# A tensor per strip, strips' rows and sums loaded once, in layer 1 of a two-layer graph network

## The chip, the cores and the metric

The kernel runs on one core of a Trainium2 chip. The metric is the time of one execution in microseconds on the device. Beside the time of a run stands the span of its profile, from the first to the last instruction; the profiled execution's time is a little longer than its span.

## The reference

Two layers over a graph of 3327 nodes with 128 features each, and a sparse 3327 x 3327 adjacency with weights. Layer 0 is a graph attention layer with four heads, layer 1 a graph convolution. Cut to what matters:

```
h = jnp.maximum(_layernorm(x, axis=-1), 0.0)
x = x + gatv2(h, adj, w1, w2, a, Wlin, w)        # per head: softmax-like weights over neighbours,
                                                 # then weights @ h @ Wlin.T, leaky relu, concat @ w
h = jnp.maximum(_layernorm(x, axis=-1), 0.0)
A_t = adj + jnp.eye(n)
D_inv = A_t.sum(axis=1) ** (-0.5)
HW = h @ W.T + b
x = x + jax.nn.relu((D_inv[:, None] * A_t * D_inv[None, :]) @ HW)
```

The change touches the last line alone: the product of the whole adjacency with HW, the scaling, the relu, and the sum with layer 0's output.

## The kernel before

**Tiles.** The nodes are padded to 3328 and cut into 26 blocks of 128 (NB = 26). Layer 0 runs block by block: for each block it gathers the neighbours' rows from a table in HBM (L595, on GpSimd), computes scores on TensorE and VectorE (L622 to L657), weighs the rows (L670, L690), and closes the block (`close`, L744 to L812). Closing block b makes its new rows xn = x + layer 0's output (L786), stores them to the HBM tensor `xn_d` (L788, from SP's queue), and puts D_inv * HW of the block into `x_sb[:, b]` (L811), from where layer 1 takes it.

**Layer 1 in strips.** Layer 1 works on strips of four blocks (512 nodes; NS = 7 strips, the last of two blocks). The sum for strip s over all columns j of the adjacency is a chain of matmuls that adds up in one PSUM bank, x_sb[:, j] times the 128 x 512 tile (s, j) of the transposed adjacency, which layer 0 left in the HBM tensor `AT_d`. A column of a strip can only be added when its block is closed. So the sum of a strip comes in three parts:

- `part1`: while block b of strip s was being prepared in layer 0, the columns that were closed by then (`finished(b)` of them: none for strip 0, 2 for strip 1, 6, 10, 14, 18, 22 for the others) were summed (`known_step`, L375) and stored to the HBM tensor `part1_d` (L387).
- `part2`: during the last two blocks of layer 0, `begin` (L920) adds twelve more columns for strips 1, 2 and 3 (L942), copies each sum out of PSUM (L947, ScalarE) into the tile `outT` and stores it to the HBM tensor `part2_d` (L948, SP).
- the rest: `layer1` (L995) goes through the list `work` of 74 pairs (s, j). The first 36 (`in_front`) are strip 0's columns 0 to 24 and strip 1's columns 14 to 24, which need no block 25; they run between the instructions that close block 25. Then come column 25 of strips 0 and 1, and strips 2 to 6. Each pair is one matmul of 128 x 512 (L1006; two records in the profile).

The 74 tiles are brought from `AT_d` in seven pieces of eleven (`strip`, L911), each into one of four buffers `g`; the DMAs of a piece alternate between SP's and GpSimd's queue (L916). A piece is fetched when the buffer's last reader is through: the fourth when the last gathered rows have been weighed (L670), the next when columns 0 to 10 are done, and so on (`allow("g")`).

**A strip's end.** `strip_in` (L955) is called some columns before a strip ends. It takes two buffers of layer 0's ring tiles, `r0` (three) and `r1` (two), and loads from SP's queue the strip's new rows (L961, from `xn_d`), its part1 (L963) and, for strips 1 to 3, its part2 (L965). `strip_out` (L968) then adds the parts to the PSUM sum (L973, L975; strip 0 has no part, there a copy on ScalarE, L977), turns the result with four transposes (L982), adds the block's own x_sb (L983), multiplies by D_inv (L984), takes the relu and adds the new rows (L985), and stores to the output from ScalarE's queue (L986). It is a generator: its first piece is emitted with the next pair of the list, its transposes two pairs later.

**What sets the order.** All of it is emitted inside `tc.manual_schedule()`: each engine executes its instructions, and each queue issues its DMAs, in the order in which the Python emits them; waits for other engines and for DMAs are put in as semaphore waits ahead of the instruction. `slot()` (L879) is called between the stages of layer 0 and moves every generator in flight by one step: closing and finishing blocks, preparation, fetching, `begin`. When the last block's groups are done, `slot()` and one pair of `layer1` alternate until all blocks are closed.

Of the kernel before, what the change touches and what calls it, by code (L numbers as in the profile page):

```python
# [231 lines left out]
def _sparse_layers(tc, nc, x, adj, w1, w2, a, wlin, w, gw, gb, gb_sb, gwT, x_sb, dinv, flag, ident, out):  # L232
# [24 lines left out]
    with ExitStack() as l0:  # L257
# [4 lines left out]
        xn_d = dram.tile([NP, D], F32, name="xn_d")  # L262
        part1_d = dram.tile([D, NP], F32, name="part1_d")
        part2_d = dram.tile([D, NP], F32, name="part2_d")
        NS = -(-NB // 4)
        TURN = NP * P + HALF
# [86 lines left out]
        def prep(b, k):  # L353
# [21 lines left out]
            def known_step(j0, js, at):  # L375
                assert all(blks[j0 + q].closed for q in js)
                pq = bank()
                for q in js:
                    nc.tensor.matmul(pq[:, :P], x_sb[:, j0 + q, :], at[:, q, :], start=(q == 0), stop=(q == js[-1]))  # L379
                yield  # L380
                if j0 == 0:
                    k.part1 = pb.tile([P, P], F32, name="part1", bufs=1)
                    nc.scalar.copy(k.part1, pq[:, :P])
                else:
                    nc.vector.tensor_add(k.part1, k.part1, pq[:, :P])
                if j0 + len(js) == finished(b):
                    nc.sync.dma_start(part1_d[:, b * P:(b + 1) * P], k.part1)  # L387
# [7 lines left out]
            SOME = 8 + 4 * 32  # L395
# [348 lines left out]
        def close(k, hb):  # L744
# [43 lines left out]
            nc.sync.dma_start(xn_d[b * P:(b + 1) * P, :], xn)  # L788
# [37 lines left out]
        NCODE = 20  # L826
        NLIST = 42
# [66 lines left out]
        strips = {}  # L894
        early = {s: range(finished(4 * s), finished(4 * s) + BEGUN) for s in (1, 2, 3) if finished(4 * s) + BEGUN < NB - 3}
# [24 lines left out]
        def begin():  # L920
# [5 lines left out]
            thirds = pa.tile([P, NP], F32, name="adjb")[:, :3 * PAIR * BANK].rearrange("p (k j i) -> p k j i", k=3, j=PAIR)  # L926

# [10 lines left out]
            for i, (s, j) in enumerate(work):  # L938
                assert blks[j].closed
                if j == early[s][0]:  # L940
                    po = bank()
                nc.tensor.matmul(po, x_sb[:, j, :], thirds[:, i // PAIR % 3, i % PAIR], start=(j == early[s][0]), stop=(j == early[s][-1]))  # L942
                if i % PAIR == PAIR - 1:
                    bring(i // PAIR + 3)
                if j == early[s][-1]:
                    part2 = pv.tile([P, H, P], F32, name="outT").rearrange("p h i -> p (h i)")
                    nc.scalar.copy(part2, po)  # L947
                    nc.sync.dma_start(part2_d[:, 4 * s * P:4 * s * P + BANK], part2)  # L948
                for _ in range(4):
                    yield  # L950
# [4 lines left out]
        def strip_in(s):  # L955

            n = min(4, NB - 4 * s)
            r0 = pr.tile([P, 2, BANK], F32, name="r0", bufs=3).rearrange("p k (b d) -> p k b d", b=4)[:, :, :n]
            r1 = pr.tile([P, 2, BANK], F32, name="r1").rearrange("p k (b d) -> p k b d", b=4)[:, :, :n]
            rows = slice(4 * s * P, (4 * s + n) * P)  # L960
            nc.sync.dma_start(r0[:, 0], xn_d[rows, :].rearrange("(b p) d -> p b d", p=P))  # L961
            if finished(4 * s):
                nc.sync.dma_start(r1[:, 0], part1_d[:, rows].rearrange("p (b i) -> p b i", b=n))  # L963
            if s in early:
                nc.sync.dma_start(r0[:, 1], part2_d[:, rows].rearrange("p (b i) -> p b i", b=n))  # L965
            return n, rows, r0, r1

        def strip_out(s, po, n, rows, r0, r1):  # L968

            ot, t, xo = r0[:, 1], r1[:, 1], r0[:, 0]  # L970
            po = po[:, :n * P].rearrange("p (b i) -> p b i", b=n)
            if s in early:
                nc.vector.tensor_add(ot, po, ot)  # L973
            if finished(4 * s):
                nc.vector.tensor_add(ot, ot if s in early else po, r1[:, 0])  # L975
            elif s not in early:
                nc.scalar.copy(ot, po)  # L977
# [5 lines left out]
            nc.vector.tensor_add(t, pt[:, :n, :], x_sb[:, 4 * s:4 * s + n, :])  # L983
            nc.vector.tensor_tensor(t, t, dinv[:, 4 * s:4 * s + n, None].to_broadcast([P, n, D]), OP.mult)  # L984
            nc.vector.scalar_tensor_tensor(xo, t, 0.0, xo, op0=OP.max, op1=OP.add)  # L985
            nc.scalar.dma_start(out[rows, :].rearrange("(b p) d -> p b d", p=P), xo)  # L986
# [8 lines left out]
        def layer1():  # L995
            ending, sums, ins = [], {}, {}
            for i, (s, j) in enumerate(work):
                if i == in_front:
                    yield "all"
                w = min(4, NB - 4 * s) * P  # L1000
                if s not in sums:
                    sums[s] = ps_z.tile([P, 2, BANK], F32, name="z")[:, 0]
                if j == min(NB - 1, first_column(s) + 4 * (s not in front)):
                    assert len(ending) < 2
                    ins[s] = strip_in(s)
                nc.tensor.matmul(sums[s][:, :w], x_sb[:, j, :], strips[s, j][:, :w], start=(j == first_column(s)), stop=(j == NB - 1))  # L1006
# [3 lines left out]
                if j == NB - 1:  # L1010
                    ending.append(strip_out(s, sums.pop(s), *ins.pop(s)))
# [370 lines left out]
```

## Time and profile before

| | us |
|---|---|
| three runs | 2480.82, 2483.68 (median), 2485.28 |
| the profiled execution's own time | 2484.15 |
| its span | 2482.0 |
| PE busy in the span | 2226.6 (90%) |
| DVE, POOL, ACT busy | 2053.7 (83%), 1769.7 (71%), 639.7 (26%) |
| layer 1's first matmul (L1006) starts at | 2388.8 |
| its last starts at | 2471.9 |
| last load of `AT_d` for layer 1 issued (SP) | 2436.01 to 2437.48 |
| last store of the output issued (ScalarE) | 2476.3 |

PE is TensorE, DVE VectorE, ACT ScalarE, POOL GpSimd and SP SyncE; PEld is the loading of weights. A name with q, as in SPq, is the engine's sequencer, which issues DMAs and waits. Rows of the timeline give the start, the length, engine, line, operation, output and inputs, how many, and in brackets the engine's idle time before it and who ended it. The mean granted clock of TensorE over the span is 0.981 of full speed. The page's row of DMA shares shows the 16 DMA engines at 90% or more in all but the last of 40 slices.

### The profile page before, as it was taken

Reading aid. Unit: us, or ns where it says so; the run is one execution under the profiler, and the core shown is the slowest. Engines: PE = TensorE matmul, PEld = TensorE weight load, DVE = VectorE, ACT = ScalarE, POOL = GpSimd, SP = SyncE. Lnnn points to the kernel's source line nnn. Section 1 sums busy time; section 2 is a strip of 40 time slices with the busy share of each in tenths; the row PEclk is TensorE's granted clock in tenths of the full one; section 3 lists DMA queues with packets and bytes.
Section 4 is the critical chain, followed back from the end, with each engine's and each line's share of the span. In section 5 each row is a group of like instructions: output and inputs, shape, how many; then the busy total and the mean of one; then the engine's idle time right before and its main releaser. Section 6 shows DMA issues by size and latency. Waiting matters only on the chain.

```text
span 2482.0 us, 51942 instructions
## 1 busy us (share of the span) xinstructions
PE 2226.6 (90%) x19254; PEld 1594.8 (64%) x19254; DVE 2053.7 (83%) x6426; ACT 639.7 (26%) x1547; POOL 1769.7 (71%) x1867
## 2 busy tenths in 40 slices
PE   6589889989988998998999999899999999999996
PEld 4466666666666766766666666666667667666653
DVE  7688988888898888889889888988988888896633
ACT  4122232223222222222222222232222222221110
POOL 3577777777777777777777777777777777777750
PEclk9799999999999999999999999999999999999998
DMA  9999999999999999999999999999999999999996
GB/s 302 381 342 332 350 333 323 352 344 316 334 368 325 323 352 334 323 345 358 324 327 360 336 323 348 353 322 338 358 329 316 354 336 319 340 334 329 367 304 174
DMA packets 401715, 826.93 MB, mean 333 GB/s; under 512 B 38435, under 2 KB 270383, under 8 KB 398127
## 3 DMA queue, kind: packets, MB, share of 16 engines
q0 software_dynamic: 144464, 628.85, 71.9%
q1 hardware_dynamic: 165343, 147.87, 18.9%
q10 hardware_dynamic: 91648, 46.80, 6.3%
q8 instruction: 155, 2.54, 0.4%
q14 instruction: 105, 0.86, 0.1%
HBM read 754.47 MB, written 113.22 MB: 350 GB/s over the span
## 4 chain that ended last, share of the span: by engine, by line
PE 41%; DVE 27%; DMA 16%; POOL 9%; issue 5%; SPq 1%; ACT 1%; DVEq 0%; POOLq 0%; ACTq 0%
DVE r L638 14%; PE z L622 14%; DMA g<-table,idx 11%; PE s L657 10%; POOL g L595 9%; DVE cand L422 3%; PE ag L670 2%; PE z L627 2%; PE tr L379 2%; DVE codes L410 1%; DVE cand L456 1%; DVE lists L453 1%; DMA g<-AT_d 1%; PE tr L942 1%; PE z L1124 1%
## 5 line engine op out<-in xcount | busy, mean ns | idle before, releaser
L595 POOL DMA_INDIRECT g<-table,idx x1664 | 1615.9, 971 | 575.1 <-issue 412.1
L638 DVE TENSOR_TENSOR r<-z,x1n 128x1024 f32<-128x1024 f32 x832 | 1010.7, 1215 | 136.5 <-PE z L622 134.4
L622 PE MATMUL z<-ident,g 128*128 128x128 f32 x6656 | 926.0, 279 | 106.9 <-DVE r L638 97.7
L622 PEld LDWEIGHTS z<-ident,g 128*128 128x128 f32 x6656 | 754.5, 143 | 244.2 <-DVE r L638 145.7
L657 PE MATMUL s<-r,sel 128*4 128x512 f32 (+1 forms) x3744 | 507.3, 582 | 9.9 <-DVE r L638 9.5
L657 PEld LDWEIGHTS s<-r,sel 128*4 128x4 f32 x3744 | 86.4, 86 | 256.2 <-issue 181.0
L698 ACT COPY ssb<-s 128x512 f32<-128x512 f32 x208 | 121.9, 586 | 497.0 <-PE s L657 496.5
L422 DVE MAX8 cand<-codes 128x8 f32<-128x52 uint16 x1664 | 217.5, 205 | 0.0
L670 PEld LDWEIGHTS ag<-g,wt 128*32 128x32 f32 x3328 | 116.7, 110 | 102.5 <-issue 95.7
L670 PE MATMUL ag<-g,wt 128*32 128x133 f32 x3328 | 158.4, 278 | 0.0
L730 ACT ACTIVATE sc<-sc 128x32 f32<-128x32 f32 x208 | 47.9, 230 | 413.3 <-DVE sc L725 252.8
L633 DVE TENSOR_TENSOR r<-z,x1n 128x128 f32<-128x128 f32 x104 | 30.1, 289 | 150.0 <-PE z L627 147.5
L367 ACT COPY at<-tr 128x512 f32<-128x512 f32 (+1 forms) x175 | 97.1, 555 | 218.0 <-PE tr L365 205.5
L453 DVE MAX8 lists<-cand 128x8 f32<-128x272 f32 (+1 forms) x338 | 133.3, 394 | 2.2
L365 PE MATMUL tr<-ident,adjb 128*128 128x128 f32 x676 | 108.4, 283 | 25.2 <-DMA adjb<-in_adj_dram 15.6
L635 ACT ACTIVATE r<-z 128x512 f32<-128x512 f32 x104 | 62.1, 597 | 256.4 <-DVE r L633 256.4
L709 PE MATMUL tr<-ident,ssb 128*128 128x128 f32 x832 | 124.9, 273 | 1.8 <-ACT ssb L698 1.8
L627 PE MATMUL z<-oi,x1b 128*128 128x256 f32 x416 | 124.3, 381 | 0.0
L595 POOL DMA_INDIRECT ge<-table,idxo x104 | 98.5, 947 | 32.9 <-issue 13.1
L456 DVE MATCH_REPLACE8 cand<-lists,cand 128x272 f32<-128x272 f32 (+1 forms) x312 | 118.0, 378 | 0.0
L410 DVE SCALAR_TENSOR_TENSOR codes<-adjb,code 128x832 uint16<-128x832 f32 x104 | 104.3, 1019 | 12.7 <-DMA adjb<-in_adj_dram 12.7
L379 PE MATMUL tr<-at,x_sb 128*128 128x128 f32 x488 | 72.2, 287 | 38.4 <-DVE sc L725 31.4
(200 smaller groups left out, 2451.8 us busy)
## 6 DMA issues: line engine op xcount, KB each, us to landing
adjb<-in_adj_dram SPq DMA_DIRECT2D x26, 1664.0 KB
table<-AT_d SPq DMA_DIRECT2D x26, 1664.0 KB
AT_d<-at ACTq DMA_DIRECT2D x150, 256.0 KB
g<-table,idx POOLq DMA_INDIRECT x1664
table<-img SPq DMA_DIRECT2D x12, 1296.0 KB
adjb<-AT_d SPq DMA_DIRECT2D x72, 128.0 KB
g<-AT_d SPq DMA_DIRECT2D x25, 256.0 KB
g<-AT_d POOLq DMA_DIRECT2D x25, 256.0 KB
```

Source lines behind the costliest of these rows:

```text
L410: nc.vector.scalar_tensor_tensor(codes[:, i], adjb[:, c0:c0 + part], 0.0, code[:, c0:c0 + part], op0=OP.not_equal, op1=OP.mult, accum_out= ...
L422: nc.vector.max(cand[:, c, 8:].rearrange("p (r s) -> p r s", s=32)[:, :, sgm % 32], codes.rearrange("p a b -> p (a b)")[:, sgm % 32 * SEG: ...
L453: nc.vector.max(top, of)
L456: nc.vector.match_replace(out=of, in_to_replace=top, in_values=of, imm_value=0.0)
L595: return nc.gpsimd.indirect_dma_start(out=g[:, t, lo:hi], out_offset=None, in_=tab, in_offset=bass.IndirectOffsetOnAxis(ap=at[:, t:t + 1], ...
L622: nc.tensor.matmul(z[:, i, q * P:(q + 1) * P], g[:, m % 2 * 4 + q, c0:c0 + D], ident, is_transpose=True, start=(q == 0 or m < 8), stop=(m ...
L627: nc.tensor.matmul(z[:, i, :n], k.x1b[:, h * D:(h + 1) * D], k.oi[:, hb * n:(hb + 1) * n], start=False, stop=True, skip_group_check=True)
L638: nc.vector.tensor_tensor(r.rearrange("p h (i s) -> p h i s", s=16), z.rearrange("p h (i s) -> p h i s", s=16), k.x1n[:, 2 * hp:2 * hp + 2 ...
L657: nc.tensor.matmul(k.s[32 * h:32 * h + 4, :n], sel[:, h, 31 - row:35 - row], r[h // 2][:, h % 2, :n], start=(row == 0), stop=(last and (m ...
L670: nc.tensor.matmul(k.ag[32 * cg:32 * cg + 32, u, :WORK], wt[:, t].rearrange("p h q -> p (h q)"), g[:, t, f0:f0 + WORK], start=(w == 0 and ...
L698: nc.scalar.copy(ssb, s)
L709: nc.tensor.transpose(pt[:, q, :], ssb[:, q * P:(q + 1) * P], ident)
```

## The change

- `xn_d` and `part1_d` become a list of HBM tensors each, one per strip, of 128 x 512, so that a strip's new rows or sums are one contiguous row per partition. The stores L387 and L788 write a 128-wide part of such a row; they stay on SP's queue.
- `part2_d` is gone. What `begin` has summed stays in SBUF, in three places that layer 0's preparation no longer uses (the tiles `codes`, `cand` and `lq`).
- `strip_in` is gone. When `layer1` starts, `places` takes four ring buffers at once (eight places of 128 x 512), one for each strip's new rows and one for strip 0's sum, and issues the loads of the new rows of strips 0 to 5 from ScalarE's queue. `parts` takes the tile `adjb`, once `begin` is through, and issues the loads of part1 of strips 1 to 6 from ScalarE's queue.
- The part2 of a strip is added to its loaded part1 in SBUF by VectorE: strip 1's four pairs before the end of the front, those of strips 2 and 3 two pairs after the strip's first column.
- The new rows of the last strip are loaded from ScalarE's queue at the first pair after the front, when block 25 is closed.
- `strip_out` has one add for a strip with a part, and works in place in the strip's two places.

The name `sums` in `layer1` becomes `acc`. The diff:

```diff
--- before.py
+++ after.py
@@ -259,10 +259,8 @@
         dram = l0.enter_context(tc.tile_pool(name="dram", bufs=1, space=bass.MemoryType.DRAM))
         tables = [dram.tile([(NP + 1) * ROW], F32, name=f"table{k}") for k in range(2)]
         hT_d = dram.tile([P, NP], F32, name="hT_d")
-        xn_d = dram.tile([NP, D], F32, name="xn_d")
-        part1_d = dram.tile([D, NP], F32, name="part1_d")
-        part2_d = dram.tile([D, NP], F32, name="part2_d")
         NS = -(-NB // 4)
+        xn_d, part1_d = ([dram.tile([P, 4 * P], F32, name=f"{name}{s}") for s in range(NS)] for name in ("xn_d", "part1_d"))
         TURN = NP * P + HALF
         AT_d = dram.tile([NB * TURN], F32, name="AT_d")
         w1_sb = res.tile([P, H, D], F32, name="w1_sb")
@@ -384,7 +382,7 @@
                 else:
                     nc.vector.tensor_add(k.part1, k.part1, pq[:, :P])
                 if j0 + len(js) == finished(b):
-                    nc.sync.dma_start(part1_d[:, b * P:(b + 1) * P], k.part1)
+                    nc.sync.dma_start(part1_d[b // 4][:, b % 4 * P:(b % 4 + 1) * P], k.part1)
 
             known = []
 
@@ -392,7 +390,6 @@
                 known[:] = [f for f in known if next(f, "end") != "end"]
 
 
-            SOME = 8 + 4 * 32
             cand = pb.tile([P, 2, SOME + 4 * 32], F32, name="cand", bufs=1)
             tab_at = 0
             while b == 0 and tab_at < NB:
@@ -785,7 +782,7 @@
             st = pb.tile([P, 1], F32, name="st")
             nc.vector.scalar_tensor_tensor(xn, x_sb[:, b, :], 1.0, py[:, 0, :], op0=OP.mult, op1=OP.add, accum_out=st)
             nc.vector.tensor_scalar(st, st, -1.0 / D, None, op0=OP.mult)
-            nc.sync.dma_start(xn_d[b * P:(b + 1) * P, :], xn)
+            nc.sync.dma_start(xn_d[b // 4][:, b % 4 * P:(b % 4 + 1) * P], xn)
             yield
 
             two = pv.tile([P, 2, D], F32, name="agn")
@@ -824,6 +821,7 @@
         ENDS = {1: (0,), 3: (1,), 5: (2,), 8: (3, 4)}
         ROWS = {1: (0, True), 3: (0, True), 5: (0, True), 7: (0, False), 8: (2, True)}
         NCODE = 20
+        SOME = 8 + 4 * 32
         NLIST = 42
         NPREP = 72
         SLOTP = 6 * 2 * NG
@@ -892,6 +890,7 @@
         PAIR = 2
         BEGUN = 12
         strips = {}
+        xs, sums, part2 = {}, {}, {}
         early = {s: range(finished(4 * s), finished(4 * s) + BEGUN) for s in (1, 2, 3) if finished(4 * s) + BEGUN < NB - 3}
 
         def columns(v, part):
@@ -924,6 +923,8 @@
             if not work:
                 return
             thirds = pa.tile([P, NP], F32, name="adjb")[:, :3 * PAIR * BANK].rearrange("p (k j i) -> p k j i", k=3, j=PAIR)
+            room = (pa.tile([P, NP // 4], F32, name="codes")[:, :BANK], pb.tile([P, 2 * (SOME + 4 * 32)], F32, name="cand", bufs=1)[:, :BANK],
+                    pb.tile([P, BANK], F32, name="lq", bufs=1))
 
             def bring(k):
                 if k < len(pairs):
@@ -943,47 +944,59 @@
                 if i % PAIR == PAIR - 1:
                     bring(i // PAIR + 3)
                 if j == early[s][-1]:
-                    part2 = pv.tile([P, H, P], F32, name="outT").rearrange("p h i -> p (h i)")
-                    nc.scalar.copy(part2, po)
-                    nc.sync.dma_start(part2_d[:, 4 * s * P:4 * s * P + BANK], part2)
+                    part2[s] = room[len(part2)].rearrange("p (b i) -> p b i", b=4)
+                    nc.scalar.copy(part2[s], po.rearrange("p (b i) -> p b i", b=4))
                 for _ in range(4):
                     yield
 
         def first_column(s):
             return early[s][-1] + 1 if s in early else finished(4 * s)
 
-        def strip_in(s):
-
-            n = min(4, NB - 4 * s)
-            r0 = pr.tile([P, 2, BANK], F32, name="r0", bufs=3).rearrange("p k (b d) -> p k b d", b=4)[:, :, :n]
-            r1 = pr.tile([P, 2, BANK], F32, name="r1").rearrange("p k (b d) -> p k b d", b=4)[:, :, :n]
-            rows = slice(4 * s * P, (4 * s + n) * P)
-            nc.sync.dma_start(r0[:, 0], xn_d[rows, :].rearrange("(b p) d -> p b d", p=P))
+        def blocks_of(s):
+            return min(4, NB - 4 * s)
+
+        def rows_of(s):
+
+            n = blocks_of(s)
+            nc.scalar.dma_start(xs[s], xn_d[s][:, :n * P].rearrange("p (b d) -> p b d", b=n))
+
+        def places():
+
+            held = [pr.tile([P, 2, BANK], F32, name=f"r{i // 3}", bufs=3 - i // 3) for i in range(4)]
+            slots = [t[:, i].rearrange("p (b d) -> p b d", b=4) for t in held for i in range(2)]
+            assert NS < len(slots)
+            xs.update((s, slots[s][:, :blocks_of(s)]) for s in range(NS))
+            if not finished(0):
+                sums[0] = slots[NS][:, :blocks_of(0)]
+            for s in range(NS - 1):
+                rows_of(s)
+
+        def parts():
+
+            of = [s for s in range(NS) if finished(4 * s)]
+            kept = pa.tile([P, NP], F32, name="adjb")[:, :len(of) * BANK].rearrange("p (s b d) -> p s b d", b=4, d=D)
+            for i, s in enumerate(of):
+                n = blocks_of(s)
+                sums[s] = kept[:, i, :n]
+                nc.scalar.dma_start(sums[s], part1_d[s][:, :n * P].rearrange("p (b i) -> p b i", b=n))
+
+        def strip_out(s, po):
+
+            n, ot, xo = blocks_of(s), sums[s], xs[s]
+            po = po[:, :n * P].rearrange("p (b i) -> p b i", b=n)
             if finished(4 * s):
-                nc.sync.dma_start(r1[:, 0], part1_d[:, rows].rearrange("p (b i) -> p b i", b=n))
-            if s in early:
-                nc.sync.dma_start(r0[:, 1], part2_d[:, rows].rearrange("p (b i) -> p b i", b=n))
-            return n, rows, r0, r1
-
-        def strip_out(s, po, n, rows, r0, r1):
-
-            ot, t, xo = r0[:, 1], r1[:, 1], r0[:, 0]
-            po = po[:, :n * P].rearrange("p (b i) -> p b i", b=n)
-            if s in early:
                 nc.vector.tensor_add(ot, po, ot)
-            if finished(4 * s):
-                nc.vector.tensor_add(ot, ot if s in early else po, r1[:, 0])
-            elif s not in early:
+            else:
                 nc.scalar.copy(ot, po)
             yield
             yield
             pt = ps_tr.tile([P, 4, P], F32, name="tr")
             for k in range(n):
                 nc.tensor.transpose(pt[:, k, :], ot[:, k, :], ident)
-            nc.vector.tensor_add(t, pt[:, :n, :], x_sb[:, 4 * s:4 * s + n, :])
-            nc.vector.tensor_tensor(t, t, dinv[:, 4 * s:4 * s + n, None].to_broadcast([P, n, D]), OP.mult)
-            nc.vector.scalar_tensor_tensor(xo, t, 0.0, xo, op0=OP.max, op1=OP.add)
-            nc.scalar.dma_start(out[rows, :].rearrange("(b p) d -> p b d", p=P), xo)
+            nc.vector.tensor_add(ot, pt[:, :n, :], x_sb[:, 4 * s:4 * s + n, :])
+            nc.vector.tensor_tensor(ot, ot, dinv[:, 4 * s:4 * s + n, None].to_broadcast([P, n, D]), OP.mult)
+            nc.vector.scalar_tensor_tensor(xo, ot, 0.0, xo, op0=OP.max, op1=OP.add)
+            nc.scalar.dma_start(out[4 * s * P:(4 * s + n) * P, :].rearrange("(b p) d -> p b d", p=P), xo)
 
 
         front = range(min(2, NS - 1))
@@ -993,22 +1006,28 @@
         pieces = [work[i:i + PIECE] for i in range(0, len(work), PIECE)]
 
         def layer1():
-            ending, sums, ins = [], {}, {}
+            ending, acc = [], {}
+            places()
             for i, (s, j) in enumerate(work):
                 if i == in_front:
                     yield "all"
-                w = min(4, NB - 4 * s) * P
-                if s not in sums:
-                    sums[s] = ps_z.tile([P, 2, BANK], F32, name="z")[:, 0]
-                if j == min(NB - 1, first_column(s) + 4 * (s not in front)):
-                    assert len(ending) < 2
-                    ins[s] = strip_in(s)
-                nc.tensor.matmul(sums[s][:, :w], x_sb[:, j, :], strips[s, j][:, :w], start=(j == first_column(s)), stop=(j == NB - 1))
+                if state["early"] is None and NS - 1 not in sums:
+                    parts()
+                for t in early:
+                    if i == work.index((t, first_column(t))) + 2 and t not in front or i == in_front - 4 and t in front:
+                        nc.vector.tensor_add(sums[t], sums[t], part2[t])
+                w = blocks_of(s) * P
+                if s not in acc:
+                    acc[s] = ps_z.tile([P, 2, BANK], F32, name="z")[:, 0]
+                if i == in_front:
+                    assert blks[NB - 1].closed
+                    rows_of(NS - 1)
+                nc.tensor.matmul(acc[s][:, :w], x_sb[:, j, :], strips[s, j][:, :w], start=(j == first_column(s)), stop=(j == NB - 1))
                 if i % PIECE == PIECE - 1 or i == len(work) - 1:
                     allow("g")
                 ending[:] = [f for f in ending if next(f, "end") != "end"]
                 if j == NB - 1:
-                    ending.append(strip_out(s, sums.pop(s), *ins.pop(s)))
+                    ending.append(strip_out(s, acc.pop(s)))
                 yield "one"
             for e in ending:
                 for _ in e:
```

## The prediction

> **What bounds the kernel now.** I read the page first, then the stretches of the span, the queue of SP in order of time, the chain of waits, and ACT and PE row by row near the end. The page gives averages over a kernel whose first 2389 us the change hardly enters; the stretches cut out the stage that it does enter.
>
> ```profile
> 2300.00:2340.00 40.00, 39.88 (x326) 26.41 (x325) 26.82 (x60) 7.59 (x23) 30.25 (x33) 1.00 1.06 364
> 2340.00:2360.00 20.00, 20.00 (x153) 13.51 (x143) 10.99 (x24) 3.71 (x10) 14.19 (x16) 1.00 1.05 368
> 2412.00:2424.00 12.00, 12.00 (x38) 5.98 (x37) 3.25 (x17) 1.31 (x5) 7.91 (x12) 1.00 1.09 291
> 2430.00:2441.00 11.00, 0.05 (x1) 0.00 (x0) 1.20 (x2) 0.00 (x0) 0.00 (x0) 0.70 1.09 298
> 2455.00:2472.00 17.00, 17.00 (x51) 8.53 (x50) 5.62 (x9) 0.00 (x0) 0.00 (x0) 1.00 0.34 105
> ```
>
> Columns: length, busy time of PE, PEld, DVE, ACT, POOL, granted clock, DMA share, GB/s. Until 2424 PE is always busy and the DMA engines are full. From 2430 to 2441 PE stands, at a clock of 0.70, while the DMA engines are still full. After 2455 PE is the bound and the DMA engines are two thirds idle. So layer 1 has one hole, of 11 us. SP's queue says why.
>
> ```profile
> 2397.15 2.69 SPq L961 DMA_DIRECT2D r<-xn_d  x1
> 2400.20 32.92 SPq L916 DMA_DIRECT2D g<-AT_d  x24
> 2433.17 0.82 SPq L961 DMA_DIRECT2D r<-xn_d  x1
> 2434.34 0.44 SPq L963 DMA_DIRECT2D r<-part_d  x1
> 2434.83 0.42 SPq L965 DMA_DIRECT2D r<-part_d  x1
> 2435.37 0.36 SPq L788 DMA_DIRECT2D xn_d<-xn  x1
> 2436.01 1.47 SPq L916 DMA_DIRECT2D g<-AT_d  x3
> ...
> 2441.24 1.11 PE L982 MATMUL tr<-ident,r 128*128 128x128 f32 x4 [11.20 <-DVE r L975]
> ```
>
> Strip 1's new rows and sums (L961, L963, L965) stand behind 24 loads of the adjacency, and PE's transposes of strip 1 wait for them. Right behind them stands the store of block 25's new rows, L788, whose data DVE had ready at 2416.3. What holds SP is in the chain of waits:
>
> ```profile
> 2402.08 7.15 DMA g<-AT_d
> 2409.24 0.02 issue
> 2409.25 0.50 SPq L916
> ...
> 2418.29 14.04 DMA g<-AT_d
> 2432.34 0.78 SPq L916
> ...
> 2434.83 4.85 DMA r<-part_d
> ```
>
> An issue at 2409.25 waited for the landing of the one at 2402.08, that at 2432.34 for the one at 2418.29: each time eight issues earlier. ACT's stores are in the same count: the first L986's semaphore wait ends at 2438.4, when the L961 of 2433.17 lands, eight DMAs before it in program order. So SP and ACT together have at most eight DMAs open.
>
> **The change, part by part.** Durations are of this execution, span 2482.0, whose time is 2484.15; the median of the runs shown is 2483.68, so I add the sum to the median.
>
> *Bytes moved ahead.* ACT issues six loads of new rows (6 x 0.262 MB) and six of sums (5 x 0.262 + 0.131 MB) when layer 1 begins, about 2389.5: 3.015 MB into full DMA engines. No row shows such loads there. Bounds: nothing, if they fill holes; 10.3 us at the 294 GB/s of 2412 to 2441. I take 8.2 us, from the 366 GB/s of 2300 to 2360, since these loads have 2 KB rows and the adjacency's have 512 B ones, nearer to the gathers of that stretch.
>
> *Bytes removed ahead of L788.* The third store of L948 at 2389.41, L961 at 2397.15, and the three of strip 1: 5 x 0.262 = 1.311 MB at 294 GB/s, 4.5 us. The other stores and loads that go lie under a full PE (2300 to 2360, 2442 to 2472) and cost nothing today.
>
> *ACT's queue.* The twelve issues come after L698 (ends 2389.5) and ahead of L730 and L732.
>
> ```profile
> 2388.91 0.58 ACT L698 COPY ssb<-s 128x512 f32<-128x512 f32 x1 [0.81 <-PE s L657]
> 2390.98 0.24 ACT L730 ACTIVATE sc<-sc 128x44 f32<-128x44 f32 x1 [1.49 <-DVE sc L727]
> ...
> 2398.87 0.66 PE L670 MATMUL ag<-g,wt 128*32 128x133 f32 x16
> ```
>
> An ACT issue takes 0.37 us (L370, 175 of them), so alone they cost 4.4 us, and L670 has that much room. But each waits for the landing eight DMAs before it. The seventh and eighth wait for the last two SP loads of the third piece, which land at 2402.5 and 2403.4 by the trace's semaphores. Then ACT is free at 2405.3 at the earliest; at 2410.3 if seven of the loads (1.84 MB, 5.0 us) push those landings back. I take 2407.5. From L730 to the end of L664 it takes 0.97 us, so L670 starts at 2408.5, 9.6 us late, and PE stands behind it in order; with 1.7 us for the half-speed start after such a hole (three z records at 0.85 for 0.43 us and four transposes at 0.21 for 0.11 after 2441) PE reaches strip 0's transposes at 2428.6 + 11.3 = 2439.9. The fourth piece's loads wait for L670 (POOL idles 6.95 us for it before 2399.86), so they start near 2409.5. By then the DMA engines have work until 2404.4 (today's landing of the L961 at 2397.15) - 1.8 (L948 and that L961) + 8.2 = 2410.8, and a load's first landing came 2.5 us after its issue in a quiet stretch (2443.31): a hole of 1.2 us, between 0 and 4.0.
>
> *The last strip's rows.* At the end of the front, ACT issues the load of strip 6 before strip 0's copy out of PSUM (now L977). That load reads what L788 stores, so it must wait for its landing; behind it on ACT stands the copy, and PE's transposes wait for the copy. L788 still stands behind SP's 24 loads. It lands now at 2435.37 + 4.85 (the neighbour's L965) = 2440.2. With 8.2 - 4.5 + 1.2 = 4.9 it lands at 2445.1. Then an issue (0.40, L986), the copy (0.59, L977) and 0.1 between: PE goes on at 2446.2, not at 2441.24: **+5.0**. Cover that is gone: today L977 runs at 2426.1, with nothing ahead of it.
>
> That ACT's later instructions stand still behind a waiting DMA is not shown on ACT in this trace, only on SP, where L963 waited 4.25 us and L961 came after it. Bounds: nothing is held (first rival), all is held; I take the second, by that row. The Trainium skill, "DMA: Bandwidth & Descriptors", section "Anatomy of one DMA", says that a DMA's semaphore wait happens on the issuing sequencer, not in the DMA engines, which speaks against putting such a load before a copy. By the page the +5.0 stands; if the page were wrong here the first rival's sum would.
>
> *After the hole.* It now comes before column (2,20) and two groups of transposes, not one: 0.86 + 0.44 = **+1.3**. The hole before the transposes at 2454.45, where the add waits for strip loads, goes: 0.96 less the usual 0.24, **-0.7**. The two adds per begun strip become one, 0.69 us of DVE, under PE's work: 0. The early adds to the sums fall where DVE idles for 3 to 4 us (before L786 and L809): 0; without that cover, 0.69 each. The copies into SBUF places instead of outT are the same copies.
>
> *Sum*: 5.0 + 1.3 - 0.7 = +5.6 us: span 2487.6, **2489.3** on the median. Own bounds: with the loads free, L788 lands at 2435.7, and PE's arrival at 2439.9 decides (second rival); with 10.3 and 4.0 for the unknowns, 9.8 in place of 4.9, +10.5.
>
> "DMA: Bandwidth & Descriptors", section "Issuing engines are not separate DMA queues", says that starting transfers from more engines saves issue time alone. It would have the moved 3.015 MB cost their full time, and at its ceiling of 435 GB/s that is an estimate of 6.9 us for 8.2, a sum of +4.3.
>
> **The rivals.** (1) ACT is not held, neither by the count of eight nor by L788. Then PE has no hole: it goes on at 2428.6 rather than 2441.24, -12.6, +1.3, -0.7, -1.7 for the half-speed start; the loads of columns (4,14) to (4,17), which land at 2432.3 today and 8.2 - 1.8 = 6.4 later, hold PE 0.2 us (it needs them at 2438.5: ten columns and three groups of transposes after 2428.6). Span 2468.5, **2470.2**: faster. For it: that the rows now come from a queue with nothing ahead. Against: the semaphore waits above. It decides if the copy L977 starts before about 2440.
>
> (2) ACT is held by the count but L788 lands before PE arrives at 2439.9, because the loads fit into the engines' time or SP's queue empties sooner. Change: -1.3 + 1.3 - 0.7 - 1.7 = -2.4, **2481.3**. Against: engines at a share of 1.05 or more in every stretch.
>
> (3) The DMA engines run dry while the fourth piece waits for L670, and the moved loads go at 294 GB/s: the upper bounds, **2494.2**. For it: the 6.95 us that POOL already waits for L670.
>
> **How the numbers follow.** Forecast 0.57, (1) 0.15, (2) 0.13, (3) 0.15. No change means within 0.2%, 5.0 us, 2478.7 to 2488.6, about what a measurement of this kernel can tell. The forecast's own spread, some 2 us either way, lies on both sides of that edge: 0.35 slower, 0.22 same. With (3) slower is 0.50; with two thirds of (2) same is 0.31; (1) and the rest give faster 0.19. The range leaves out (1) and the far end of (3): 2477 to 2495.
>
> **What would show it.** Right: L730 starts after 2403 with PE idle before L670; the strip 6 load on ACT issued within 0.1 us of L788's landing, L977's successor right behind it, and PE's long hole before strip 0's transposes. The moved loads' cost shows in L788's issue, later than 2435.4. Wrong: L730 still near 2391 (no count of eight); the copy near 2426 (no wait on ACT); a hole under 3 us in PE after 2424.

## The result, and the profile after

| | before | after |
|---|---|---|
| median of 17 runs each, us | 2482.99 | 2489.0 |
| lowest and highest | 2474.55, 2486.12 | 2485.96, 2491.89 |
| profiled execution, its span | 2484.15, 2482.0 | 2490.95, 2489.2 |
| layer 1, first matmul to the span's end | 93.2 | 102.2 |

The ratio is 1.0027, with a 95% interval of 1.0021 to 1.0034: slower, by 6.0 us. Four of the later kernels ran on a chip on which layer 0 took some 900 us longer, that of the kernel before too (3385.7 us), so those four are compared by the length of layer 1. TensorE's holes in layer 1 were shorter on that chip, so they are compared only with each other.

SP's queue in order of time, in the kernel after:

```profile
2367.36 69.18 SPq L915 DMA_DIRECT2D g<-AT_d  x39
2436.64 1.89 SPq L785 DMA_DIRECT2D xn_d<-xn  x1
2438.84 3.18 SPq L915 DMA_DIRECT2D g<-AT_d  x3
```

The store of block 25's new rows (L785, L788 before) is still behind the adjacency's loads. Strip 1's loads are no longer there.

ScalarE in the same stretch; the brackets hold the idle time ahead and what ended it:

```profile
2387.13 0.58 ACT L695 COPY ssb<-s 128x512 f32<-128x512 f32 x1 [0.81 <-PE s L654]
2390.20 11.99 ACTq L961 DMA_DIRECT2D r<-xn_d  x6
2402.31 3.41 ACTq L981 DMA_DIRECT2D adjb<-part_d  x6
2405.77 0.24 ACT L727 ACTIVATE sc<-sc 128x44 f32<-128x44 f32 x1 [18.05 <-DMA adjb<-part_d]
2434.07 0.40 ACT L808 ACTIVATE x_sb<-agn,dinv 128x128 f32<-128x128 f32 x1 [4.92 <-DVE one L1357]
2443.84 0.33 ACTq L961 DMA_DIRECT2D r<-xn_d  x1
2444.21 0.58 ACT L990 COPY r<-z 128x512 f32<-128x512 f32 x1 [9.74 <-DMA xn_d<-xn]
```

Twelve loads keep ScalarE from 2390.2 to 2405.7, and the tanh of the last scores (L727) comes only then. The thirteenth load waits until 2443.84 for the store to land; the copy of strip 0's sum (L990), which needs nothing from the store, waits with it. A row that reads "L990 waits for xn_d" is thus a queue's order, not a dependence of the copy.

What TensorE makes of it:

```profile
2388.42 8.75 PE L1025 MATMUL z<-g,x_sb 128*128 128x512 f32 x20
2406.79 1.11 PE L667 MATMUL ag<-g,wt 128*32 128x133 f32 x16 [9.63 <-DVE wt L661]
...
2434.52 1.99 PE L1025 MATMUL z<-g,x_sb 128*128 128x512 f32 x4 [0.36 <-ACT x_sb L808]
2444.85 3.78 PE L1025 MATMUL z<-g,x_sb 128*128 128x512 f32 x4 [8.34 <-ACT r L990]
2448.42 1.06 PE L995 MATMUL tr<-ident,r 128*128 128x128 f32 x4
2449.27 1.71 PE L1025 MATMUL z<-g,x_sb 128*128 128x512 f32 x2
2450.82 0.60 PE L995 MATMUL tr<-ident,adjb 128*128 128x128 f32 x4
```

There are two holes where there was one, 9.63 us ahead of the weighing (L667) and 8.34 us ahead of column 18 of strip 2; the one of 11.20 us before strip 1's transposes is gone. Columns 18 and 19 of strip 2 then take 3.57 us instead of 1.72, as the next view shows by the granted clock: the stretches of the span, with the columns of the table in the prediction.

```profile
2397.17:2406.79 9.62, 0.00 (x0) 0.00 (x1) 0.48 (x2) 0.48 (x2) 0.00 (x0) 0.62 1.05 327
2406.79:2412.00 5.21, 5.21 (x33) 3.26 (x34) 1.80 (x6) 0.00 (x0) 3.77 (x7) 0.72 0.90 298
2436.50:2444.85 8.35, 0.01 (x2) 0.01 (x1) 0.69 (x1) 0.58 (x1) 0.00 (x0) 0.73 1.06 280
2444.85:2455.00 10.15, 10.15 (x23) 4.97 (x24) 4.66 (x7) 0.00 (x0) 0.00 (x0) 0.71 0.15 41
2455.00:2472.00 17.00, 17.00 (x47) 7.95 (x46) 6.73 (x10) 0.00 (x0) 0.00 (x0) 1.00 0.17 47
```

In both holes the DMA engines are full (1.05 and 1.06), so they look like a lack of bandwidth; after the second they are nearly idle (0.15) while TensorE works at a granted clock of 0.71. The experiments ask whether bytes or order made the holes.

### The profile page after: what moved, and what is told of

Same layout as the page of the kernel before. It is cut to its first block, busy times and chain, and to the rows that moved or that the text cites. A ratio compares the mean times of both kernels' runs of the same rounds, so it can differ in the third digit from the quotient of the medians.

```text
span 2489.2 us, 51919 instructions
## 1 busy us (share of the span) xinstructions
PE 2228.5 (90%) x19254; PEld 1594.2 (64%) x19254; DVE 2051.7 (82%) x6426; ACT 639.5 (26%) x1547; POOL 1770.0 (71%) x1867
## 4 chain that ended last, share of the span: by engine, by line
PE 42%; DVE 26%; DMA 13%; POOL 11%; issue 6%; SPq 1%; ACT 1%; DVEq 0%; ACTq 0%; POOLq 0%
PE z L619 14%; DVE r L635 14%; PE s L654 10%; POOL g L592 10%; DMA g<-table,idx 10%; DVE cand L419 3%; PE ag L667 2%; PE z L1025 2%; PE z L624 2%; PE tr L377 2%; DVE cand L453 1%; DVE codes L407 1%; DVE lists L450 1%; PE tr L943 1%; DMA adjb<-in_adj_dram 1%
## 5 line engine op out<-in xcount | busy, mean ns | idle before, releaser
L667 PEld LDWEIGHTS ag<-g,wt 128*32 128x32 f32 x3328 | 117.3, 111 | 113.7 <-issue 96.7
L667 PE MATMUL ag<-g,wt 128*32 128x133 f32 x3328 | 159.6, 280 | 9.6 <-DVE wt L661 9.6
L727 ACT ACTIVATE sc<-sc 128x32 f32<-128x32 f32 x208 | 47.9, 230 | 431.1 <-DVE sc L722 257.4
L619 PE MATMUL z<-ident,ge 128*128 128x128 f32 x416 | 82.7, 281 | 26.4 <-DVE r L635 26.4
```

The costliest lines, as they stand in the source:

```text
L619: nc.tensor.matmul(z[:, i, q * P:(q + 1) * P], g[:, m % 2 * 4 + q, c0:c0 + D], ident, is_transpose=True, start=(q == 0 or m < 8), stop=(m ...
L667: nc.tensor.matmul(k.ag[32 * cg:32 * cg + 32, u, :WORK], wt[:, t].rearrange("p h q -> p (h q)"), g[:, t, f0:f0 + WORK], start=(w == 0 and ...
```

## The experiments

The theory was that of the prediction: ScalarE is held twice in its own order, by the count of eight open DMAs and by the store's landing. Against it stood these: the moved 3 MB fill the DMA engines, from whatever queue they come; the size of the loads, not their count, holds ScalarE; the new layout of the tensors, or the freeing of SP's queue alone, makes the difference.

**One wait at a time.** The thirteenth load alone goes to GpSimd's queue:

```diff
-            nc.scalar.dma_start(xs[s], xn_d[s][:, :n * P]...
+            (nc.gpsimd if s == NS - 1 else nc.scalar).dma_start(xs[s], xn_d[s][:, :n * P]...
```

> The changed kernel, with the load of the last strip's new rows issued from GpSimd's queue, where nothing stands behind it, instead of ScalarE's; the other twelve loads stay on ScalarE. Theory (two waits on ScalarE, of which the second decides): the copy of strip 0 no longer waits for block 25's store, PE's hole of 8.3 us before column (2,18) goes, with it the half-speed start of 3 us: -11.3 us against the changed kernel, 2477.7 us, 5 us below the kernel before. PE's hole of 9.6 us before the weighing (L667) stays. Rival (the 3.0 MB put ahead of the adjacency cost the time on the DMA engines, wherever they are issued): the hole turns into waits for the adjacency's tiles, 2489 us.

Measured: 2478.67 us, 0.9983 [0.9971, 0.9994] of the kernel before. TensorE's rows in it:

```profile
2406.24 1.11 PE L667 MATMUL ag<-g,wt 128*32 128x133 f32 x16 [9.34 <-DVE wt L661]
...
2434.01 3.79 PE L1025 MATMUL z<-g,x_sb 128*128 128x512 f32 x8 [0.36 <-ACT x_sb L808]
2437.63 0.60 PE L995 MATMUL tr<-ident,r 128*128 128x128 f32 x4
```

The second hole is gone, and columns 25 of two strips and 18 and 19 of the third run on in one row; the first hole stays. The store landed 57.5 us after layer 1's first matmul, later than in the kernel after (56.8): nothing that TensorE needs waits for it now.

Then the reverse, the first twelve to GpSimd and the thirteenth on ScalarE:

```diff
-            nc.scalar.dma_start(xs[s], ...
+            (nc.scalar if s == NS - 1 else nc.gpsimd).dma_start(xs[s], ...
...
-                nc.scalar.dma_start(sums[s], ...
+                nc.gpsimd.dma_start(sums[s], ...
```

> The changed kernel, with the twelve early loads issued from GpSimd's queue and the last strip's load left on ScalarE. Theory: the tanh of block 25 (L727) runs near 2390 again, the hole of 9.6 us before the weighing goes, but the copy of strip 0 still waits for block 25's store, which stands behind the same bytes: the hole before column (2,18) grows to some 18 us and the time stays, 2487 to 2489 us. Rival (the count of eight is the whole cost, the last load costs nothing): -11 us, 2478 us.

Measured: 2488.86 us, 1.0022 [1.0011, 1.0034]. Rows of ScalarE, SP and TensorE:

```profile
2392.35 0.24 ACT L727 ACTIVATE sc<-sc 128x44 f32<-128x44 f32 x1 [1.49 <-DVE sc L724]
...
2440.57 0.77 SPq L785 DMA_DIRECT2D xn_d<-xn  x1
...
2444.98 0.34 ACTq L961 DMA_DIRECT2D r<-xn_d  x1
2445.36 0.59 ACT L990 COPY r<-z 128x512 f32<-128x512 f32 x1 [19.07 <-DMA xn_d<-xn]
...
2446.00 3.78 PE L1025 MATMUL z<-g,x_sb 128*128 128x512 f32 x4 [17.67 <-ACT r L990]
```

The tanh is on time and the first hole gone, and nearly nothing is won: TensorE arrives earlier at a copy that still waits for the store, and the hole there grows from 8.34 to 17.67 us. The two waits lie one behind the other, so the gain of the pair is not the sum of the two.

Both at once, all thirteen loads from GpSimd's queue:

```diff
-            nc.scalar.dma_start(xs[s], ...
+            nc.gpsimd.dma_start(xs[s], ...
...
-                nc.scalar.dma_start(sums[s], ...
+                nc.gpsimd.dma_start(sums[s], ...
```

> All thirteen loads from GpSimd's queue. Theory: both holes go, PE is the bound from 2387 to the end, with at most 2 us of waiting for the tiles of columns (4,14) to (4,17): 2468 us (2466 to 2471). Rival (bytes): 2485 to 2489 us.

Measured: **2469.32 us, 0.9949 [0.9932, 0.9966]**, the best of all, faster than both kernels. Layer 1 takes 81.7 us. GpSimd's row of the thirteenth load and TensorE's rows:

```profile
2440.96 0.55 POOL L961 DMA_DIRECT2D r<-xn_d  x1 [14.67 <-DVE adjb L996]
```

```profile
2419.61 4.89 PE L1025 MATMUL z<-g,x_sb 128*128 128x512 f32 x10
2424.33 0.60 PE L995 MATMUL tr<-ident,r 128*128 128x128 f32 x4
...
2432.78 2.81 PE L1025 MATMUL z<-g,x_sb 128*128 128x512 f32 x6 [2.26 <-DMA g<-AT_d]
```

The store lands 55.9 us after the first matmul, 0.9 us from where it did, and the same bytes are moved at the same stage; 19.7 us less than the kernel after (19.4 by the two ratios to the kernel before) come from the queue of issue alone. GpSimd waits 14.67 us ahead of the thirteenth load, but has nothing due behind it. The twelve are not free there: GpSimd's half of the fourth piece of the adjacency stands behind them, and its first load left 16.1 us after the first matmul, against 11.1 in the kernel before. What is left, 2.26 us, is a wait for an adjacency tile from SP's queue (issued at 2417.52, landed at 2432.65); whether it follows from that delay is not shown.

**Is the queue enough?** The kernel before, with only its three loads of a strip moved from SP to GpSimd:

```diff
-            nc.sync.dma_start(r0[:, 0], xn_d[rows, :]...
+            nc.gpsimd.dma_start(r0[:, 0], xn_d[rows, :]...
-                nc.sync.dma_start(r1[:, 0], part1_d[:, rows]...
+                nc.gpsimd.dma_start(r1[:, 0], part1_d[:, rows]...
-                nc.sync.dma_start(r0[:, 1], part2_d[:, rows]...
+                nc.gpsimd.dma_start(r0[:, 1], part2_d[:, rows]...
```

> The kernel before, with nothing changed but the queue of the strips' loads: new rows, part1 and part2 go from GpSimd's queue instead of SP's. Theory (the hole of 11 us before the change is SP's queue alone): strip 1's parts are issued before 2425, PE has no hole after 2424: -11.7 for the hole, -1.7 for the half-speed start, -0.7 for the later wait: 2469 us (2467 to 2472). Rival (the DMA engines are the bound there, the loads only end last because all do): 2479 us or more, with waits for the adjacency's tiles in place of the hole.

Measured: 2480.85 us, 0.999 [0.9977, 1.0002]; the forecast was 12 us too low. TensorE's three rows, and GpSimd's waits (line, what it waited for, us in total, how many, the longest):

```profile
2430.76 0.66 PE L982 MATMUL tr<-ident,r 128*128 128x128 f32 x4 [1.37 <-DVE r L975]
2441.42 1.09 PE L982 MATMUL tr<-ident,r 128*128 128x128 f32 x4 [3.14 <-DVE r L975]
2452.66 1.11 PE L982 MATMUL tr<-ident,r 128*128 128x128 f32 x4 [4.32 <-DVE r L975]
```

```profile
POOL r L963 <- DVE r L985: 21.8, 3, 9.0
POOL r L961 <- DMA out_dram<-r: 14.3, 3, 9.5
```

The one hole becomes three smaller ones. The first waits for strip 1's last load (L965), which landed at 2429.19. Behind the other two stand the ring buffers: the sums of strip 2 go into one that strip 0 holds until its last sum (L985), and the new rows of strip 3 into one that strip 0 holds until the store of its output is through. The same waits stood in SP's queue in the kernel before:

```profile
SPq L963 <- DVE r L985: 14.6, 3, 6.0
SPq L961 <- DMA out_dram<-r: 10.4, 3, 3.7
```

There they came after the one long hole, and TensorE had no wait over 1 us for them. So places of their own are worth something once the queue is free: 2480.85 against 2469.32 is 11.5 us on the same queue. That difference holds the rest of the change too (the sums that stay in SBUF, the earlier loads), which no run here parts from the places.

**Count or bytes?** The twelve loads are cut to 32 of 128 partitions, a quarter of the bytes, all still on ScalarE; GpSimd sets the rest to zero, so the strips' rows and sums are incomplete:

```diff
-            nc.scalar.dma_start(xs[s], xn_d[s][:, :n * P]...
+            part = slice(0, P if s == NS - 1 else 32)
+            nc.scalar.dma_start(xs[s][part], xn_d[s][part, :n * P]...
...
-                nc.scalar.dma_start(sums[s], part1_d[s][:, :n * P]...
+                nc.scalar.dma_start(sums[s][:32], part1_d[s][:32, :n * P]...
```

> The changed kernel, with the twelve early loads cut to 32 of 128 partitions, a quarter of the bytes (the other rows of those places are set to zero by GpSimd, so strips' rows and sums are incomplete). Theory (each ScalarE issue waits for the landing eight DMAs before it): ScalarE is still held until the third piece's SP loads land, L727 runs 15 us after layer 1's first matmul or later (18.8 in the changed kernel, 2.2 before), and the hole before the weighing is still 6 us or more; the store lands some 6 us earlier: about 2482 us. Rival (the issues are slow because the engines are full of these very bytes): the hole falls to 2.5 us or less, L727 within 8 us.

Measured: layer 1 98.0 us (time 3391.13, 1.0012 [0.9991, 1.0032]). Rows of ScalarE and TensorE:

```profile
3300.10 5.74 ACTq L962 DMA_DIRECT2D r<-xn_d  x6
3305.96 9.35 ACTq L987 DMA_DIRECT2D adjb<-part_d  x6
3315.36 0.24 ACT L727 ACTIVATE sc<-sc 128x44 f32<-128x44 f32 x1 [14.68 <-DMA adjb<-part_d]
...
3316.39 1.11 PE L667 MATMUL ag<-g,wt 128*32 128x133 f32 x16 [6.26 <-DVE wt L661]
```

With a quarter of the bytes ScalarE is still held for 15.2 us; the tanh comes 15.38 us after the first matmul, and TensorE stands 6.3 us before the weighing. The 18.75 and 9.6 us of the kernel after are of another chip. On this one ran the kernel of the next experiment, whose twelve loads are whole and stand where they stand in the kernel after:

```profile
3269.91 4.15 ACTq L961 DMA_DIRECT2D r<-xn_d  x6
3275.85 8.13 ACTq L981 DMA_DIRECT2D adjb<-part_d  x6
3284.03 0.24 ACT L727 ACTIVATE sc<-sc 128x44 f32<-128x44 f32 x1 [13.54 <-DMA r<-xn_d]
...
3285.05 1.12 PE L667 MATMUL ag<-g,wt 128*32 128x133 f32 x16 [5.12 <-DVE wt L661]
```

The whole loads held ScalarE for 14.1 us, with the tanh at 14.24 and a hole of 5.1 us, no longer than a quarter of their bytes. So nothing here puts this wait down to the size of the loads. In the trace seven of the twelve small loads start 0.02 to 0.08 us after the landing of the DMA eight before them, as the count of eight has it.

**The store's queue.** Block 25's store moves from SP to GpSimd, the rest as in the kernel after; it ran twice, on the chip with the long layer 0 and again on another:

```diff
-            nc.sync.dma_start(xn_d[b // 4]...
+            (nc.gpsimd if b == NB - 1 else nc.sync).dma_start(xn_d[b // 4]...
```

> The changed kernel, with block 25's store of new rows (L785) issued from GpSimd's queue instead of SP's; the load of the last strip's rows stays on ScalarE ahead of the copy. Theory (ScalarE waits for that store, and the store for its place in SP's queue): GpSimd issues it near 2430, it lands near 2436, the copy of strip 0 runs near 2437, the hole before column (2,18) shrinks from 8.3 to about 1 us and the half-speed start of 3 us goes: 2478 us. Rival (the DMA engines' bytes are what is late, whatever the queue): 2487 us or more.

> The changed kernel with block 25's store on GpSimd's queue, as in e4_store, whose layer 1 took 89.2 us. Theory: 89 to 91 us, 2478 us. Rival (bytes): 2487 us or more.

Measured: layer 1 89.2 us in the first, 93.6 in the second; times 3393.11 (1.0015 [0.9991, 1.0039]) and 2486.06 (1.0015 [1.0004, 1.0026]). The second, on GpSimd and ScalarE:

```profile
2426.28 0.56 POOL L785 DMA_DIRECT2D xn_d<-xn  x1
```

```profile
2435.54 0.33 ACTq L961 DMA_DIRECT2D r<-xn_d  x1
2435.91 0.59 ACT L990 COPY r<-z 128x512 f32<-128x512 f32 x1 [3.38 <-DMA g<-AT_d]
```

The store is issued eight us earlier after the first matmul (41.7 against 49.6) and lands 6.5 us after its issue, at 2432.82. ScalarE's load leaves only at 2435.54, 0.08 us after the landing of the adjacency load eight DMAs before it: the count of eight again, and not the store, holds the copy, for 3.38 us. The hole falls to 2.0 us. The forecast of the time missed: this profiled execution took 2480.27, but the kernel's twelve executions lie between 2477.5 and 2489.47, and their median is 2.3 us below the kernel after on the same chip. Why they scatter stays open.

**The loads later.** The twelve loads come at the seventh pair of `work` instead of ahead of the first, the thirteenth three pairs later, all on ScalarE; this one too ran on both chips:

```diff
-            places()
             for i, (s, j) in enumerate(work):
...
-                if state["early"] is None and NS - 1 not in sums:
+                if i == 6:
+                    places()
                     parts()
...
-                if i == in_front:
+                if i == in_front + 3:
                     assert blks[NB - 1].closed
                     rows_of(NS - 1)
```

> The changed kernel, all thirteen loads still from ScalarE's queue, but later in the order: the twelve at the seventh pair, behind tanh and exp (L727, L729), the last strip's rows at the third pair behind the front, after the copy of strip 0. Theory (what stands behind the waiting load is the whole cost): both holes go; the twelve end near 18 us after layer 1's first matmul, when the next instruction of ScalarE (L751) is due at 14.3, under PE's columns: 2470 us (2467 to 2473). Rival (ScalarE's queue is wrong, as its issues are counted with SP's): 2478 us or more.

> The changed kernel with the thirteen loads on ScalarE later in the order (twelve at the seventh pair, the last three pairs behind the front), as in e6_later, whose layer 1 took 80.1 us. Theory: 80 to 82 us for layer 1, 2468 us, 0.6% below the kernel before. Rival (ScalarE's queue is wrong whatever the order): 2478 us or more.

Measured: layer 1 80.1 and 87.4 us, times 3377.38 (0.9985 [0.9965, 1.0006]) and 2474.77 (0.9967 [0.9954, 0.998]). Rows of the second, ScalarE and then TensorE:

```profile
2388.93 11.70 ACTq L961 DMA_DIRECT2D r<-xn_d  x6
2401.20 4.38 ACTq L981 DMA_DIRECT2D adjb<-part_d  x6
2405.63 0.63 ACT L751 ACTIVATE agn<-ag,rec 128x128 f32<-128x128 f32 x2 [17.41 <-DMA g<-AT_d]
```

```profile
2429.13 3.75 PE L1025 MATMUL z<-g,x_sb 128*128 128x512 f32 x4 [4.16 <-DMA g<-AT_d]
```

The tanh and the copy are ahead of the loads they had been held by, and both holes are gone. That a place in the order helps on the same queue shows the wait, not ScalarE's queue, to be the cost. The forecast of 2468 missed by 7 us: a hole of 4.16 us for an adjacency tile takes their place in the second run, which the first did not have, and the matmuls behind it lose 2.6 us more at a lower clock; together that is most of the 7.3 us between the two runs' layer 1. The twelve loads still take 16.7 us to issue, and they delay SP through the common count: seven of SP's adjacency loads, from 2405.89 to 2420.74, each left 0.02 us after the landing of one of the twelve, eight DMAs before. The tile that TensorE waited for left SP at 2418.91, right behind one of these, and landed at 2429.00.

**Layout, and repeats.** The kernel before with a tensor per strip and nothing else of the change (its essential lines):

```diff
-            nc.sync.dma_start(xn_d[b * P:(b + 1) * P, :], xn)
+            nc.sync.dma_start(xn_d[b // 4][:, b % 4 * P:(b % 4 + 1) * P], xn)
...
-            nc.sync.dma_start(r0[:, 0], xn_d[rows, :]...
+            nc.sync.dma_start(r0[:, 0], xn_d[s][:, :n * P]...
```

> The kernel before, with one tensor per strip for new rows and part1 and nothing else changed. Theory: the same time as before, within 3 us. Rival (the layout, with rows of 2 KB for 512 B, or the waits between strips' stores and loads, is what matters): 5 us or more off.

Measured: 3383.1 us, 0.9997 [0.9976, 1.0017]; layer 1 91.9 us with the hole still there, at 8.8. The time leaves some 7 us either way open on this chip; by the length of layer 1, no longer than that of the kernel before on other chips (93.2, and 94.8 below), the layout by itself gives no sign of making the change slower.

Both kernels as they were, once more:

> The kernel before, once more with a profile. Layer 1 took 93.2 us from its first matmul to the end of the span in the first profile, that of the changed kernel 102.2, 9.0 more, while the times differ by 6.0. Theory (layer 0 varies from one execution to the next, layer 1 does not): 93 us again, within 1 us, with another start. Rival (layer 1 of the first profile was an unlucky one): 95 us or more. Time 2483 us.

> The changed kernel, once more with a profile. Theory: layer 1 takes 102 us, within 1 us; what the difference of times lacks to 9 us is layer 0, which starts layer 1 some 2 to 3 us earlier on the average. Rival: 99 to 100 us. Time 2489 us.

Measured: 2482.03 (1.0 [0.999, 1.001]) with layer 1 at 94.8 us, and 2488.31 (1.0034 [1.0022, 1.0046]) with layer 1 at 102.0 and holes of 9.8 and 6.7. The first is 0.8 us outside the expected 92 to 94: its hole is 11.5 us, and the matmuls behind it lose 2.9 us at a lower clock, against 1.7 in the first profile. Layer 1 is thus about 8 us longer, and the time 6.

## Why the prediction was right, point by point

The time was forecast at 2489.3 us and came out at 2489.0, slower in sign and from the forecast's own case: both waits on ScalarE were there, and TensorE went on within 0.4 us of the forecast. That the total agrees to 0.3 us is luck: what comes after the hole took 3 us more than the sum has, and layer 1 began earlier, for which the sum has no term. Times below count from layer 1's first matmul (2388.8 before, 2387.0 after).

| step | before | forecast | after |
|---|---|---|---|
| tanh starts (L730, now L727) | 2.2 | 18.7 | 18.75 |
| hole before the weighing | 0 | 9.6 | 9.63 |
| `x_sb` of block 25 written (L808 after) | 36.1 | 47.4 | 47.5 |
| block 25's store landed | 51.1 | 56.3 | 56.8 |
| TensorE goes on | 52.4 | 57.4 | 57.8 |
| from there to the span's end | 40.76 | 41.4 | 44.35 |

*ACT's queue* was right, and the experiment with a quarter of the bytes shows the count behind it. The trace of the kernel after shows it as well: the six issues of L961 start at 2390.20, 2391.79, 2396.71, 2400.08, 2401.04 and 2401.86, each 0.02 to 0.08 us after the landing of the DMA eight before it in program order.

*The last strip's rows* were right: the load left ScalarE when the store landed, and the copy followed 0.37 us later. This is what the Trainium skill, "DMA: Bandwidth & Descriptors", section "Anatomy of one DMA", says of a DMA's semaphore wait, that it happens on the issuing sequencer. The 9.74 us ahead of L990 agree, and add that on ScalarE an instruction that needs nothing from the DMA waits behind it.

*Bytes moved ahead and removed*: the store landed 5.7 us later, and was forecast 0.5 us earlier than that. Of the 5.7, 3.05 us are in its issue (49.63 against 46.58) and 2.62 in its flight (7.17 us against 4.55); the forecast didn't part the two. Its "hole of 1.2 us" in the DMA engines' work is only a dip: their share falls to 0.70 in the us from 2408 to 2409.

*After the hole* is the term that was mis-sized: "+1.3" and "-0.7", but the rest of layer 1 grew by 3.6 us, not 0.6. The prediction put the hole ahead of strip 0's transposes, behind columns 18 and 19 of strip 2. But strip 2's sum needs a buffer of `z`, of which there are two, and strip 0's copy frees one; so the hole is ahead of column 18, and two columns more (1.7 us) come after it. And the half-speed stretch was longer: 3.57 us for 1.72 (two columns), 0.85 for 0.44 (four transposes) and 1.55 for 0.86 (one column), each from start to next start, make 2.95 us, where it costs 1.7 before and the prediction left that as it stood; 1.25 more. 1.3 + 1.7 + 1.25 - 0.7 = 3.55. These 1.25 us are not the change's doing: the kernel before lost 2.9 us when it was run again.

*What made up for it*: layer 1 began earlier. The change's kernels have their first matmul at 2386.1 on average (seven profiles, 2384.4 to 2390.2), those built on the kernel before at 2388.0 (three, 2387.0 to 2388.8). 2387.0 - 2388.8 = -1.8, and +9.0 - 1.8 = 7.2 is the difference of the spans. The prediction had no term for layer 0. That the stores of part2 are gone would fit; it wasn't tried, and seven profiles that spread over 6 us don't settle it, so the cause stays open.

The rivals: (1), that ScalarE isn't held, is false, but its price was right for a kernel in which nothing is: 2470.2 forecast, 2469.32 with all loads on GpSimd. (2), that the store lands before TensorE arrives, is false by 7 us: TensorE was through column 25 of the first two strips at 49.5 and stood, and the store landed at 56.8. (3), that the DMA engines run dry while the fourth piece waits, is false: in none of the stretches above, from layer 1's start to the end of the second hole, was their share below 0.90.

The Trainium skill, "DMA: Bandwidth & Descriptors", section "Issuing engines are not separate DMA queues", holds that more issuing engines save issue time only. Here the same bytes from another engine's queue moved the time by 19.7 us, not through bandwidth but through what stood behind the waiting issues.

## What to carry to other kernels

Before a load is put on a compute engine's queue, read what that engine has to do next and who waits for it: a load that must wait for a store, or for a free place among the open DMAs, holds all of that. Put it on a queue, or at a place in the order, with nothing due behind it, and give it a buffer of its own; here neither the queue (2480.85) nor the change with its buffers (2489.0) helped alone, and the two together gave 2469.32. When two waits lie one behind the other, take both away before judging either: removing the first alone gave 0.1 us, after the second it gave 9.4.

## What the runs showed of the hardware

- In these programs SP and ScalarE together had at most eight DMAs open, so a queue that had issued nothing for long was still held by the other's transfers: for 15.2 us with a quarter of the bytes and for 14.1 us with all of them, on one chip. In the traces the DMAs of these two queues take eight completion semaphores in turn, and each waits for the last use of its own; GpSimd's take eight others.
- After a hole of 8.34 us TensorE's matmuls took about twice their time for some 6 us: 2.95 us lost, at a granted clock of 0.71 over 10 us. The loss is not set by the hole's length nor by what comes first after it: with the same instructions behind a hole of 17.67 us it was 2.0 us, and two runs of the kernel before, with holes of 11.20 and 11.52 us, lost 1.7 and 2.9.
- GpSimd's queue paces its issues by landings too: in the fastest kernel its twelve loads left at 2388.66 to 2400.05, with gaps that ended 0.28 to 0.55 us after the landing of its DMA eight before. TensorE did not stand there, as neither the tanh nor the copy is GpSimd's.
- The same programs took some 900 us longer in layer 0 on one chip and about the same in layer 1 (91.9 us with per-strip tensors, against 93.2 and 94.8 of the kernel before elsewhere), with shorter holes: 5.1 against 9.6 us before the weighing with the store on GpSimd, the same kernel on two chips. What made that chip differ wasn't tried.
